# A tuned float32 layer kernel: its warm-up reads a constant, gate's weight comes in two loads, and the first products go by halves of the inputs

## The chip, the cores and the metric

The kernel runs on one core of one Trainium2 chip. The metric is the device time of one execution in microseconds (us). The kernel before took 528.29 us, the median of three runs (527.94 to 528.46).

## The reference

The input `x` is (4, 2048, 256) in float32, so 8192 tokens of 256 features. A layer is chunked linear attention with a gate, a residual and a layer norm, and then a gated feed-forward network with integer weights, a residual and a second layer norm. Cut to what is computed:

```python
Q, K, V = x @ W_q.T, x @ W_k.T, x @ W_v.T
mask = where(diff >= 0, decay ** diff, 0)          # inside chunks of 32 tokens; decay = sigmoid(log_decay[0])
S = einsum('bncd,bnkd->bnck', Qc, Kc) * mask
O = einsum('bnck,bnkd->bncd', S, Vc).reshape(B, T, D)
gate = sigmoid(x @ W_g.T)
x = layernorm(x + (gate * O @ W_o.T + x))          # attention adds its own x as well
h = silu(x @ wg.T) * (x @ wu.T)                    # wg, wu, wd: integers of -127..127, times 1/127
x = layernorm(x + h @ wd.T)
```

## The kernel before

The 8192 tokens are worked on in 16 blocks of 512 (`TB`). Activations are held with the features in the partitions (`xT`, two chunks of 128 features by 512 tokens) for the products, and with the tokens in the partitions for the norms. The scores use the product M of W_q and W_k (`m_sb`, made once by `make_m`), so that one projection `yT` takes the place of Q and K. From block 1 on, gate, y, v and the output projection are split into seven half-size products (`seven`, `split_gate`, `token_sums`, `weight_sums`), with the sums of quarters made by GpSimd. The feed-forward products use the weights in two kinds, as float32r (`hi`) and float16 (`lo`). The last two blocks have a hand-written tail. A branch at the end, `wide_block`, handles integers too large for float16; with these inputs it is not entered, though it calls `attn_gate` too.

The work of all blocks is overlapped in one long program per engine. A scheduler puts the instructions of each engine in order; those given to `in_turn` (`tc.keep_in_program_order`) keep the order of the program.

What matters here is the head, before the loop over the blocks begins at line 938:

- **Loads.** `load_w(nc.scalar, w_gT, "wg")` (line 138) issues gate's weight, 256 KB, as the first instruction of ScalarE's queue. On SyncE's queue (SP) `load_xT(0, pieces=KD)` issues block 0's `xT` in two loads of 256 KB, one for each chunk of 128 features. Behind `wg` on ScalarE's queue stand `wv`, `decay` and `wk`; behind `xT_0` on SP stand `wq`, `xT_1` (512 KB), `wo`, the two blocks of `x` and nine pieces of the integer weights. The loads from SP and ScalarE share eight completion semaphores, which are given out in turn; a load that takes one again waits for the load that had it.
- **Warm-up.** Lines 174 to 178: VectorE writes a tile `idle` of 128 by 512 zeros, and TensorE multiplies it twice (`WARM`) into a bank that nobody reads. Each float32 product appears in the trace as two pieces.
- **First products.** `attn_gate(0)` (line 889) makes gate of block 0: for each half `dc` of the output features, two products over the input chunks `ec`, then ScalarE's sigmoid of that bank. `attn_v(0)` follows with `wv`, then `make_m` with `wq` and `wk`, then `split_gate(1, x_sums)`, whose sums GpSimd makes from `xT_1`, and `attn_y(0)`.
- **Sigmoid of decay.** ScalarE's first computing instruction is the sigmoid of `decay` (line 205); the sigmoids of gate stand behind it on that engine. VectorE builds the mask from `decay`.

Constants such as zeros are also there without a tile of the kernel's own: the program's first instructions, GpSimd memsets ahead of the barrier that starts all engines, lay down one column of each.

Of the kernel before, what the change touches and what calls it, by code (L numbers as in the profile page):

```python
# [47 lines left out]
F32 = mybir.dt.float32  # L48
# [6 lines left out]
P = 128  # L55
# [3 lines left out]
TB = 512  # L59
# [12 lines left out]
def kernel(  # L72
# [15 lines left out]
    nc = tc.nc  # L88
    NT, D = x.shape
    H = ffn_gT.shape[1]  # L90
    KD = D // P
# [4 lines left out]
    const = ctx.enter_context(tc.tile_pool(name="const", bufs=1))  # L96
# [12 lines left out]
    def bank(name):  # L109
        return psum.tile([P, TB], F32, tag="ps", name=name)  # L110
# [5 lines left out]
    def load_xT(b, start=None, pieces=1):  # L116
        xt = xin.tile([P, KD, TB], F32, tag="xT", name=f"xT_{b}")
        src = xT[:, span(b, start)].rearrange("(k p) t -> p k t", p=P)
        n = KD // pieces
        for k in range(0, KD, n):  # L120
            nc.sync.dma_start(xt[:, k : k + n, :], src[:, k : k + n, :])
        return xt
# [3 lines left out]
        nc.sync.dma_start(xn, x[span(b, start), :].rearrange("(g p) d -> p g d", p=P))  # L126
        return xn

    def load_w(eng, w, name):
        k, n = w.shape[0] // P, w.shape[1]  # L130
        t = const.tile([P, k, n], w.dtype, tag=name, name=name)
        eng.dma_start(t, w.rearrange("(k p) n -> p k n", p=P))
        return t


    decay = const.tile([P, 1], F32, tag="decay", name="decay")
    xTs, xns = {}, {}
    wg = load_w(nc.scalar, w_gT, "wg")
    xTs[0] = load_xT(0, pieces=KD)
    wv = load_w(nc.scalar, w_vT, "wv")  # L140
    nc.scalar.dma_start(decay, log_decay[0:1, 0:1].to_broadcast([P, 1]))
    wq = load_w(nc.sync, w_q, "wq")
    wk = load_w(nc.scalar, w_k, "wk")
    xTs[1] = load_xT(1)
# [26 lines left out]
    ]  # L171


    idle = const.tile([P, TB], F32, tag="idle", name="idle")
    nc.vector.memset(idle, 0.0)
    pi = bank("pi")
    for _ in range(WARM):
        nc.tensor.matmul(pi, lhsT=idle[:, :P], rhs=idle, start=True, stop=True)  # L178

    ident = const.tile([P, P], F32, tag="ident", name="ident")  # L180
    make_identity(nc, ident)
# [108 lines left out]
    def in_turn(ins):  # L290
        tc.keep_in_program_order(ins)
# [260 lines left out]
    def attn_gate(b):  # L552
        xt = xTs[b]
        sg = work.tile([P, KD, TB], F32, tag="sg", name=f"sg_{b}")
        for dc in range(KD):
            pg = bank(f"pg_{b}_{dc}")
            for ec in range(KD):
                nc.tensor.matmul(  # L558
                    pg,
                    lhsT=wg[:, ec, dc * P : (dc + 1) * P],  # L560
                    rhs=xt[:, ec, :],
                    start=(ec == 0),
                    stop=(ec == KD - 1),
                )
            nc.scalar.activation(sg[:, dc, :], pg, AF.Sigmoid)
        return sg

# [245 lines left out]
    def ffn_down(b, uT, h, between=None, chunkwise=False):  # L813


        r = work.tile([P, NG, D], F32, tag="r2", name=f"r2_{b}")
        mv = no_moments(f"f{b}")
        made = None
        order = in_turn if chunkwise else free

        def residual(gs, pb):

            order(
                nc.vector.scalar_tensor_tensor(  # L824
                    flat(r, gs), pb, SCALE**3 / U_UP * H_UP, flat(h, gs), ALU.mult, ALU.add
                )
            )
            nonlocal made
            moments(r, f"f{b}", range(gs.start, gs.stop), order, mv)
            if between is not None and gs.start == 0:  # L830
                made = between()

        ws = [chunked(w) for w in fd]
        if chunkwise:
            per = TB // D
            banks = [bank(f"fdn_{b}_{k}") for k in range(NG // per)]
            for late, terms in enumerate(early_and_late(uT, ws)):
                for k, pb in enumerate(banks):
                    for i, (part, w) in enumerate(terms):
                        for j in range(per):  # L840
                            g = k * per + j
                            product = nc.tensor.matmul(  # L842
                                pb[:, j * D : (j + 1) * D],
                                lhsT=part[:, g * P : (g + 1) * P],
                                rhs=w,
                                start=late + i + j == 0,
                                stop=True,
                                skip_group_check=True,
                            )
                            in_turn(product)  # L850
                    if late:
                        residual(slice(k * per, (k + 1) * per), pb)
        else:
            project_back(b, uT, ws, residual, "fdn")
        return r, mv, made
# [31 lines left out]
    table = const.tile([P, 1], F32, tag="table", name="table")  # L887
    hs, hTs = {}, {}
    sg, v = attn_gate(0), attn_v(0)
    for w, name in ((wg, "g"), (wv, "v")):  # L890
        w_sums[name] = weight_sums(w, name)
# [46 lines left out]
    for b in range(NB - 2):  # L938
        n = b + 2
# [67 lines left out]
        else:  # L1007
# [14 lines left out]
            r_out, mv_out, _ = ffn_down(b, uT, hs.pop(b), chunkwise=True)  # L1022
# [6 lines left out]
    per = NG // 2  # L1029
# [26 lines left out]
    r_before, mv_before, _ = ffn_down(last - 1, uT, hs[last - 1], chunkwise=True)  # L1056
# [28 lines left out]
    banks = [bank(f"fdn_{last}_{g}")[:, :D] for g in range(NG)]  # L1085
# [42 lines left out]
    def wide_block(start, weights):  # L1128

        wide_g, wide_u, wide_d = weights  # L1130
        xTs["w"] = load_xT("w", start)
        xns["w"] = load_xn("w", start)
        sg, v = attn_gate("w"), attn_v("w")
        goT = attn_values("w", attn_scores("w", attn_y("w")), v, sg)
        h = attn_out("w", goT)
# [41 lines left out]
    with tc.If(wide_any > 0):  # L1177
# [10 lines left out]
        for w in (ffn_gT, ffn_uT, ffn_dT):  # L1188
            weights.append([])
            for src in int_pieces(w):  # L1190
                t = room.pop(0).rearrange("p (k n) -> p k n", n=D)
# [47 lines left out]
```

## Time and profile before

| | |
|---|---|
| median of 3 runs | 528.29 us (527.94 to 528.46) |
| the profiled execution, its time | 527.63 us |
| its span in the profile | 525.9 us |
| granted TensorE clock, mean | 0.995 |
| TensorE busy from 0 to 60 us, outside of the first 1.45 | all of it |
| TensorE busy from 500 to 525.9 us | 18.74 of 25.90 us |
| weight `wg`: issue, time to landing | 0.73 us, 4.4 us |
| `xT_0`, first half | 0.73 us, 3.7 us |
| `xT_0`, second half | 1.18 us, 4.7 us |
| `xT_1` | 2.11 us, 8.8 us |
| `wk` | 2.26 us, 8.9 us |

The span is what the profile shows from the first to the last instruction; the time of a run includes 1.73 us around it. PE is TensorE's matmuls, PEld its weight loads, DVE VectorE, ACT ScalarE, POOL GpSimd and SP SyncE. Start times are us from the beginning of the span. The times to landing are those from the start of a load's issue to the moment all of its data is there.

### The profile page before, as it was taken

What the parts mean: (1) busy time and instruction counts of PE and PEld (TensorE: products, weight loads), DVE (VectorE), ACT (ScalarE), POOL (GpSimd) and SP (SyncE); (2) the same over time, 40 slices, a digit from 0 to 9 for tenths busy, and PEclk for the clock granted to TensorE, in tenths of its full rate; (3) what the DMA queues carried; (4) which work ended last, traced back from release to release, by engine and by line L of the source; (5) the groups of instructions that cost most, each with busy time, mean ns of one, the idle gap of its engine ahead of it and who ended that gap; (6) DMA issues with size and microseconds to landing.
All of it is one profiled execution on the core that took longest, in us unless ns stands there. A gap on an engine that the chain in (4) does not pass through costs nothing.

```text
span 525.9 us, 10552 instructions
## 1 busy us (share of the span) xinstructions
PE 517.3 (98%) x3646; PEld 422.2 (80%) x3646; DVE 389.8 (74%) x964; ACT 322.3 (61%) x644; POOL 343.2 (65%) x476
## 2 busy tenths in 40 slices
PE   8999999999999999999999999999999999999994
PEld 5798887887978788887887978788887888878683
DVE  3878797686786867777677776867868677787865
ACT  2745565465656756666575655666666575667744
POOL 6535785766847668585776857668485675735653
PEclk9999999999999999999999999999999999999998
DMA  7721121213213131131312313141131312011201
GB/s 252 218 91 42 51 60 28 65 42 67 96 34 87 53 110 41 39 109 31 105 42 51 112 30 92 49 113 41 36 93 51 105 42 53 30 27 54 79 22 65
DMA packets 43256, 36.90 MB, mean 70 GB/s; under 512 B 4800, under 2 KB 39104, under 8 KB 43200
## 3 DMA queue, kind: packets, MB, share of 16 engines
q1 hardware_dynamic: 42240, 35.41, 23.2%
q8 instruction: 30, 0.49, 0.4%
q10 hardware_dynamic: 960, 0.79, 0.4%
q14 instruction: 26, 0.21, 0.2%
HBM read 20.45 MB, written 8.39 MB: 55 GB/s over the span
## 4 chain that ended last, share of the span: by engine, by line
PE 95%; DVE 2%; ACT 1%; POOL 1%; issue 0%; DVEq 0%; ACTq 0%
PE fg L776 16%; PE fu L776 16%; PE fdn L663 14%; PE p_v L462 9%; PE p_y L444 9%; PE p_g L444 9%; PE p_o L462 8%; PE po L637 5%; PE ps L616 3%; PE fdn L842 2%; PE pa L663 1%; PE pg L558 1%; PE pi L178 1%; PE pv L596 1%; PE py L575 1%; DVE st_f L311 0%
## 5 line engine op out<-in xcount | busy, mean ns | idle before, releaser
L801 POOL TENSOR_TENSOR u_lo<-u,u_hi 128x512 f16<-128x512 f32 (+1 forms) x98 | 123.0, 1257 | 111.0 <-ACT u_hi L800 109.6
L800 ACT CAST u_hi<-u 128x512 fp32r<-128x512 f32 (+1 forms) x98 | 59.7, 609 | 65.3 <-DVE u L798 64.9
L786 DVE SCALAR_TENSOR_TENSOR s<-fg,s 128x512 f32<-128x512 f32 (+1 forms) x98 | 65.9, 673 | 34.3 <-ACT s L784 34.1
L784 ACT ACTIVATE s<-fg 128x512 f32<-128x512 f32 (+1 forms) x98 | 56.9, 583 | 41.5 <-PE fg L776 41.4
L798 DVE TENSOR_TENSOR u<-fu,s 128x512 f32<-128x512 f32 (+1 forms) x98 | 66.4, 678 | 10.4 <-POOL u_lo L801 1.1
L776 PE MATMUL fg<-hT_hi,fg_hi 128*128 128x512 f32 (+1 forms) x196 | 74.0, 458 | 0.0
L776 PE MATMUL fu<-hT_hi,fu_hi 128*128 128x512 f32 (+1 forms) x196 | 60.5, 390 | 0.0
L776 PE MATMUL fg<-hT_lo,fg_lo 128*128 128x512 f16 (+1 forms) x196 | 58.0, 377 | 0.0
L776 PE MATMUL fu<-hT_lo,fu_lo 128*128 128x512 f16 (+1 forms) x196 | 57.4, 375 | 0.0
L663 PE MATMUL fdn<-fd_hi,u_hi 128*128 128x256 f32 x312 | 46.9, 292 | 0.0
L776 PEld LDWEIGHTS fu<-hT_hi,fu_hi 128*128 128x128 f32 x196 | 36.5, 188 | 8.5
L399 ACT ACTIVATE h<-h,shift_h,scale_h 128x256 f32<-128x256 f32 x52 | 27.0, 590 | 24.1 <-POOL shift_h L362 24.1
L776 PEld LDWEIGHTS fg<-hT_hi,fg_hi 128*128 128x128 f32 x196 | 34.6, 189 | 8.8
L663 PEld LDWEIGHTS fdn<-fd_hi,u_hi 128*128 128x128 f32 x312 | 39.8, 189 | 0.3
L663 PE MATMUL fdn<-fd_lo,u_lo 128*128 128x256 f16 x312 | 38.6, 273 | 0.0
L776 PEld LDWEIGHTS <-fu_lo 128*128 128x128 f16 x196 | 19.2, 98 | 22.2
L824 DVE SCALAR_TENSOR_TENSOR r<-fdn,h 128x512 f32<-128x512 f32 x30 | 20.7, 689 | 21.6 <-PE fdn L663 19.1
L759 POOL TENSOR_TENSOR hT_lo<-hT,hT_hi 128x512 f16<-128x512 f32 x28 | 35.3, 1280 | 1.2 <-ACT hT_hi L758 1.2
L776 PEld LDWEIGHTS <-fg_lo 128*128 128x128 f16 x196 | 15.3, 98 | 20.7 <-issue 12.9
L663 PEld LDWEIGHTS <-u_lo 128*128 128x128 f16 x312 | 28.4, 98 | 4.2
L462 PE MATMUL p_v<-v_sums,x_sums 128*128 128x128 f32 x240 | 31.7, 275 | 0.0
L637 PE MATMUL po<-sT,v 128*128 128x128 f32 x256 | 31.2, 275 | 0.0
(207 smaller groups left out, 1183.0 us busy)
## 6 DMA issues: line engine op xcount, KB each, us to landing
x<-in_x_dram SPq DMA_DIRECT2D x16, 512.0 KB, 3.5
xT<-in_xT_dram SPq DMA_DIRECT2D x15, 512.0 KB, 4.3
hT<-sq SPq DMA_DIRECT2D x224, 32.0 KB, 1.9
out_dram<-r SPq DMA_DIRECT2D x14, 512.0 KB, 5.0
fg_int<-in_ffn_gT_dram SPq DMA_DIRECT2D x3, 256.0 KB, 7.8
fu_int<-in_ffn_uT_dram SPq DMA_DIRECT2D x3, 256.0 KB, 7.0
fd_int<-in_ffn_dT_dram SPq DMA_DIRECT2D x3, 256.0 KB, 5.9
xT<-in_xT_dram SPq DMA_DIRECT2D x2, 256.0 KB, 4.2
```

The lines of the kernel that those rows point to most:

```text
L399: nc.scalar.activation(r[:, g, :], r[:, g, :], AF.Identity, bias=shift[:, g : g + 1], scale=scale[:, g : g + 1],)
L444: nc.tensor.matmul(pb, lhsT=a[i - 1], rhs=b[i - 1], start=first, stop=True, skip_group_check=True,)
L462: nc.tensor.matmul(pb[:, g * P : (g + 1) * P], lhsT=b[i - 1][:, g * P : (g + 1) * P], rhs=a[i - 1], start=first and g == 0, stop=True, ski ...
L637: nc.tensor.matmul(po[:, cols], lhsT=v[:, g, dc * P : (dc + 1) * P], rhs=sT[:, cols], start=True, stop=True,)
L663: nc.tensor.matmul(pb[:, j * D : (j + 1) * D], lhsT=part[:, g * P : (g + 1) * P], rhs=w, start=(i == 0), stop=(i == len(terms) - 1),)
L759: nc.gpsimd.tensor_tensor(in_order[1], whole, in_order[0].bitcast(F32), ALU.subtract)
L776: nc.tensor.matmul(pb, lhsT=w[kind][:, dc, hc * P : (hc + 1) * P], rhs=hT[kind][:, dc, cols], start=(kind == kinds[0] and dc == 0), stop=( ...
L784: order(nc.scalar.activation(s, pg, AF.Sigmoid, scale=SCALE / H_UP))
L786: gated = nc.vector.scalar_tensor_tensor(s, pg, U_UP / H_UP**2, s, ALU.mult, ALU.mult)
L798: in_steady_turn(nc.vector.tensor_tensor(u, pu, s, ALU.mult))
L800: nc.scalar.copy(hi, u)
L801: nc.gpsimd.tensor_tensor(lo, u, hi.bitcast(F32), ALU.subtract)
```

## The change

Three edits. `load_w` takes a number of pieces, and gate's weight is issued as two loads of 128 KB, one for each input chunk. The tile `idle` and its memset are gone; both operands of the warm-up products read the constant zero, one element repeated over the free dimension. In `attn_gate` the loop over the input chunks becomes the outer one: both banks get the product of the first chunk, then both get that of the second, in this order on TensorE; the two sigmoids come after all four products.

```diff
-    def load_w(eng, w, name):
+    def load_w(eng, w, name, pieces=1):
         k, n = w.shape[0] // P, w.shape[1]
         t = const.tile([P, k, n], w.dtype, tag=name, name=name)
-        eng.dma_start(t, w.rearrange("(k p) n -> p k n", p=P))
+        per = k // pieces
+        for i in range(0, k, per):
+            eng.dma_start(
+                t[:, i : i + per, :], w.rearrange("(k p) n -> p k n", p=P)[:, i : i + per, :]
+            )
         return t
...
-    wg = load_w(nc.scalar, w_gT, "wg")
+    wg = load_w(nc.scalar, w_gT, "wg", pieces=KD)
...
-    idle = const.tile([P, TB], F32, tag="idle", name="idle")
-    nc.vector.memset(idle, 0.0)
     pi = bank("pi")
     for _ in range(WARM):
-        nc.tensor.matmul(pi, lhsT=idle[:, :P], rhs=idle, start=True, stop=True)
+        nc.tensor.matmul(
+            pi,
+            lhsT=nc.const_aps.tensor(0.0, [P, P]),
+            rhs=nc.const_aps.tensor(0.0, [P, TB]),
+            start=True,
+            stop=True,
+        )
...
-        for dc in range(KD):
-            pg = bank(f"pg_{b}_{dc}")
-            for ec in range(KD):
-                nc.tensor.matmul(
+        banks = [bank(f"pg_{b}_{dc}") for dc in range(KD)]
+
+        for ec in range(KD):
+            for dc, pg in enumerate(banks):
+                product = nc.tensor.matmul(
                     pg,
                     lhsT=wg[:, ec, dc * P : (dc + 1) * P],
                     rhs=xt[:, ec, :],
                     start=(ec == 0),
                     stop=(ec == KD - 1),
                 )
+                in_turn(product)
+        for dc, pg in enumerate(banks):
             nc.scalar.activation(sg[:, dc, :], pg, AF.Sigmoid)
```

On each engine the order of instructions is otherwise that of before. One thing follows from the extra load without being in the diff: with eight semaphores in turn, the ninth load of the program, the first that takes one again, was `wo` and is now `xT_1`.

## The prediction

> **What bounds the kernel now.** I read the page first (busy shares, then the chain that ended last), then the chain in order of time over the first 20 us, the windows, and last the head instruction by instruction. In the page the reader sees TensorE busy for 98% of the span and carrying 95% of the chain:
>
> ```profile
> span 525.9 us, 10552 instructions
> PE 517.3 (98%) x3646; PEld 422.2 (80%) x3646; DVE 389.8 (74%) x964; ACT 322.3 (61%) x644; POOL 343.2 (65%) x476
> PE 95%; DVE 2%; ACT 1%; POOL 1%; issue 0%; DVEq 0%; ACTq 0%
> ```
>
> In the windows (stretch, its length, then busy time of PE, PEld, DVE, ACT, POOL) PE's busy time equals the length of the stretch: after 1.45 us TensorE has no gap until the tail.
>
> ```profile
> 1.45:5.23 3.78, 3.78 (x5) 1.21 (x5) 0.24 (x2) 1.28 (x1) 1.44 (x6) 1.00 0.84 266
> 5.23:9.10 3.87, 3.87 (x9) 1.94 (x10) 0.07 (x1) 0.30 (x2) 3.87 (x9) 1.00 0.68 209
> 60.00:500.00 440.00, 440.00 (x3126) 360.89 (x3125) 332.28 (x801) 278.04 (x551) 295.95 (x391) 1.00 0.22 62
> ```
>
> The chain in order of time (start, length, what) says what TensorE does first. Only the 0.72 us before the start, the memset of `idle` and the warm-up lie ahead of real work:
>
> ```profile
> 0.72 0.18 issue
> 0.91 0.50 DVE idle L175
> 1.40 0.04 issue
> 1.45 3.78 PE pi L178 x4
> 5.23 3.83 PE pg L558 x8
> 9.06 3.45 PE pv L596 x16
> 12.52 1.73 PE pm L194 x8
> ```
>
> The timeline of the head shows that the first real weight load waits for a transfer and not for the warm-up (in brackets: idle time before, and releaser):
>
> ```profile
> 2.46 0.34 PEld L178 LDWEIGHTS pi<-idle 128*128 128x128 f32 x1 [0.52 <-issue]
> 3.32 0.34 PEld L178 LDWEIGHTS pi<-idle 128*128 128x128 f32 x1 [0.52 <-issue]
> 5.19 0.47 PEld L558 LDWEIGHTS pg<-xT,wg 128*128 128x128 f32 x2 [1.54 <-DMA wg<-in_w_gT_dram]
> 5.90 0.19 PEld L558 LDWEIGHTS pg<-xT,wg 128*128 128x128 f32 x1 [0.24 <-DMA xT<-in_xT_dram]
> 10.99 0.85 POOL L433 TENSOR_TENSOR x_sums<-xT 128x256 f32<-128x256 f32 x1 [1.38 <-DMA xT<-in_xT_dram]
> ```
>
> A float32 product is two pieces on the array. The warm-up's four start at 1.45, 2.46, 3.31 and 4.17, 0.86 apart, so the array is through at 4.17 + 0.86 = 5.03. The weight `wg` lands 4.4 us after its issue at 0.73, at 5.13, and the first load starts at 5.19. From there the eight gate pieces come 0.43 apart. Landing times of the others, issue plus time to landing: first half of `xT_0` 0.73 + 3.7 = 4.43, second half 1.18 + 4.7 = 5.88, `wv` 6.52, `wq` 8.74, `decay` 8.74, `xT_1` 10.91, `wk` 11.16.
>
> **What the Trainium skill says.** "TensorE: Matmul & The Clock Gate", Part 1: The HAM clock gate: an idle array runs at half clock and is released after a busy window of 3413 ns, and the window is free-running, so the moment varies between executions. The trace agrees in kind: 0.86 us a piece first, 0.43 later. The first gate weight load took 302 ns where cold ones took 338 and warm ones 190, so the clock rose at about 5.45, 4.0 us after TensorE's first work. "DMA: Bandwidth & Descriptors", Queues, rings and completion order: the queues of SyncE and ScalarE each have a ring on the same 16 engines, which take turns between them packet by packet. The trace agrees: `wg` and the halves of `xT_0` move side by side at 353 GB/s together from 3.25 to 5.75. The pages price no matmul operand that reads one element over and over.
>
> **The change, part by part.**
>
> *Warm-up from the constant.* POOL writes the constant at 0.25, ahead of the start barrier, so nothing after 0.72 holds the warm-up back. Its start is 0.72 plus TensorE's own issue: 0.76 with the 0.04 of the chain, 0.91 if it is as slow as VectorE. I take 0.85, 0.60 earlier. Four pieces then end at 0.85 + 3.58 = 4.43. The repeated read of one element is not in the trace: not faster, since the array clock sets 0.86; at worst twice 0.86, which would end the warm-up near 7.9. I take 0.86, because the number of columns is the same and the values are zeros in both; the other end is left to the chance of slower. VectorE loses a memset of 0.48 us in front of 7.34 us of idleness (its next work waits for `decay`): nothing.
>
> *Gate's weight in two loads.* At 353 GB/s shared by two queues a load gets about 176 GB/s, so the second 128 KB take 0.74 us, and the first half lands at 5.13 - 0.74 = 4.39 (bounds 4.1 and 4.8). The second still lands near 5.13. One more issue on ScalarE's queue, 0.4 to 0.5 us, moves `wv`, `decay` and `wk` back in issue by that much. Their landings are set by the ring, which is busy until well after their issue, so I take 0.1 (0 to 0.45). Behind the issues stand the table load (1.28 us at 2.75, then 4.76 us idle) and the sigmoid of `decay`; the gate's sigmoids stand behind that one, at 8.99. Cover: `wv` is needed at about 7.9; `wk` at 12.14 - 0.6 = 11.54 against 11.16, so 0.38 us is free.
>
> *An indirect wait.* Each load takes one of eight completion semaphores in turn. Before, the ninth load was `wo`, which waits for the first load and so went out at 5.17. With one load more the ninth is `xT_1`: the list of waits of the changed kernel shows it behind semaphore 0, which is the first half of `wg`. Its issue moves from 2.11 to about 4.45, and on SP `wo`, both `x` and nine weight pieces stand behind it. But its data waited anyway: it follows `wq` in SP's ring, and `wq` lands at 8.74. Issue to first data was about 1 us for the first load, so descriptors are there at 5.5, in time. I take 0; bounds 0 and 2.34 (the whole issue delay). GpSimd's sums (four of some 0.75 us) hang on it. The product that needs the third of them, ready at 13.26, would come at 13.9: 0.64 us are free. `wo` and what follows go out within 0.3 us of before.
>
> *Products by halves.* Same eight pieces, same order on the engine afterwards. The first four need only the first halves: max(4.43 warm-up, 4.43 `xT_0`, 4.39 `wg`) + 0.06 = 4.49 instead of 5.19, saving 0.70. The other four come 1.7 us or more later, after 5.88. Both sigmoids now follow all eight pieces, finished by about 8.3, and wait for `decay` at 8.74 as before: nothing.
>
> *Clock.* The exposed cold weight load stays, so products stream from 4.80. If the clock rises 4.0 us after the start again (4.85), they lose 0.03; if it rises at 5.45 as before, they are cold for 0.65 us and lose half, 0.33. Sum: 0.67 or 0.37. I take 0.55, nearer the first, because the execution shown lost next to nothing to cold products and a random window treats both kernels alike.
>
> Profiled execution: 525.9 - 0.55 = 525.35 span; with the 1.73 around it (527.63 - 525.9) 527.1. The median, 528.29, lies 0.66 above that execution, so the forecast is 528.29 - 0.55 = **527.7**. About 0.2% (1.06 us) is what a measurement of this kernel can tell from no change, so this counts as no change.
>
> **Rivals.**
>
> *The gain is swallowed (528.2).* The clock rises where it did and `wk` lands 0.4 late. For: only 0.38 us of cover. Against: ring and not issue sets landings. 0.37 less a wait of some 0.3 leaves 0.1.
>
> *Clearly faster (526.9).* If the weight load is hidden and all pieces are warm, gate ends at 4.49 + 8 x 0.43 = 7.93 instead of 8.90, a gain of 0.97; and the median's surplus of 0.66 may be cold products, which an earlier warm-up removes in part. 0.97 + 0.4 gives 1.4. Against: it wants a lucky clock, and `xT_0` at 4.43 and `wk` at 11.16 cap it.
>
> *Slower (529.4): `xT_1` behind the new wait.* If its landing moves by the whole 2.34, x_sums' consumer stalls 2.34 - 0.64 - 0.6 (already gained) = 1.1 beyond the old time. It decides from a delay of 1.24, where the kernel is even; slower by 0.2% needs 2.3. For: DMA share falls to 0.38 between 5.75 and 7.50, so the rings do run dry there. Against: in that stretch `wq` and `decay` are ahead of it.
>
> *The warm-up doesn't do its work*, because it reads one zero: the first products run cold, or the warm-up itself lasts to 7.9; either costs 1 to 3 us and is part of the chance of slower.
>
> **How the numbers follow.** Forecast 0.56, swallowed 0.15, faster 0.20, slower 0.09. The first two are within 0.2%: 0.71. Range 526.9 to 528.7: it takes in the swallowed case, the bounds 0.37 and 0.97, a few tenths of spread between executions (527.94 to 528.46 shown), and the nearer half of the faster case; the slower case stays out.
>
> **What would show it.** First warm-up piece near 0.85 and released by no memset; first gate load near 4.5 with `wg` or `xT` as releaser; `pv` from about 8.2 to 8.5 instead of 8.90; `pm` near 11.6 without a wait for `wk`; `xT_1` issued near 4.45, landing by 11; PE without gaps later. Wrong if `x_sums` starts after 12, if gate pieces stay 0.86 apart past 6, or if PE shows idle time between 9 and 15.

## The result, and the profile after

The changed kernel takes 527.20 us (median of 22 runs, 526.65 to 528.07) against 528.06 for the kernel before, measured beside it (22 runs, 527.29 to 528.87). The ratio is 0.9986 with a 95% interval of 0.998 to 0.9992: 0.74 us won, between 0.42 and 1.06. (The two medians alone are 0.86 apart; gains are given here by the ratio.) A second measurement of the same kernel (e4 below) gave 0.9985 (0.9978 to 0.9991). So the gain is real, at about 0.14%.

The one profile of after, taken alone, seems to say the opposite. Its page:

```profile
span 526.3 us, 10554 instructions
PE 517.9 (98%) x3646; PEld 422.4 (80%) x3646; DVE 390.1 (74%) x963; ACT 322.3 (61%) x644; POOL 342.5 (65%) x476
```

The span is 0.4 us longer than that of before. The chain in order of time (start, length, what) shows where the head stands:

```profile
0.67 0.06 issue
0.73 3.89 DMA wg<-in_w_gT_dram
4.62 0.04 issue
4.66 4.53 PE pg L567 x8
9.20 3.45 PE pv L607 x16
12.65 1.73 PE pm L202 x8
```

The memset and the warm-up have left the chain: it now begins with the first half of gate's weight, which lands at 4.62. (In other profiles of kernels with this head, such as those of e3 and e4, it begins with the warm-up: the two end within a few tenths of a microsecond of each other.) Gate's products follow it at 4.66, 0.53 us earlier than before (5.19). But they take 4.53 us instead of 3.83, so `pv` starts at 9.20, 0.14 later than before (9.06). The weight loads in the timeline say why:

```profile
0.74 0.50 PEld L180 LDWEIGHTS pi<-const-float32-0.0 128*128 128x128 f32 x2 [0.74 <-issue]
1.76 0.34 PEld L180 LDWEIGHTS pi<-const-float32-0.0 128*128 128x128 f32 x1 [0.52 <-issue]
2.61 0.34 PEld L180 LDWEIGHTS pi<-const-float32-0.0 128*128 128x128 f32 x1 [0.52 <-issue]
4.66 0.50 PEld L567 LDWEIGHTS pg<-xT,wg 128*128 128x128 f32 x2 [1.72 <-DMA wg<-in_w_gT_dram]
5.68 0.34 PEld L567 LDWEIGHTS pg<-xT,wg 128*128 128x128 f32 x1 [0.52 <-issue]
6.46 0.19 PEld L567 LDWEIGHTS pg<-xT,wg 128*128 128x128 f32 x1 [0.44 <-issue]
6.89 0.19 PEld L567 LDWEIGHTS pg<-xT,wg 128*128 128x128 f32 x1 [0.24 <-issue]
```

A load of 0.34 us is one at half clock, one of 0.19 at full clock. The warm-up starts at 0.74 to 0.77 instead of 1.45, and its pieces are 0.86 apart with the constant as with the tile. In this execution the clock rose near 6.3 us. In the profiled execution of before it rose near 5.6: the line `5.19 0.47`, shown in the prediction, covers two loads, and the one that took 302 ns is the second of them, from 5.36 to 5.66; it was at half clock for about 0.26 us of that (0.338 us is a cold load, 0.190 a warm one). Real work was thus cold (at half clock) for some 1.3 us here, from 5.0 to 6.3, and for next to nothing there. After the head the windows show TensorE without a gap, as before:

```profile
30.00:60.00 30.00, 30.00 (x239) 25.43 (x238) 22.88 (x61) 16.61 (x36) 19.07 (x30) 1.00 0.22 72
60.00:500.00 440.00, 440.00 (x3125) 360.92 (x3125) 332.16 (x802) 278.05 (x552) 295.56 (x391) 1.00 0.22 62
```

The chain gives a ruler for all runs of this study. From the start of `py` in it to the start of the last normalising instruction on VectorE (line 875 of before, 886 of after) it is 504.83 us in before and 504.77 in after. The two lines of before, then those of after:

```profile
15.97 3.43 PE py L575 x8
520.80 0.41 DVE r L875
```

```profile
16.10 3.43 PE py L586 x8
520.87 0.41 DVE r L886
```

In the other nine profiles whose chain runs over `py` it is 504.77 to 504.82. What the head wins or loses arrives at the end to within 0.06 us. The rest of the scatter lies behind it: from that instruction to the end of the timed run it is 6.8 to 7.6 us, in code that the change leaves as it was.

### The profile page after: what moved, and what is told of

Same layout as the page of the kernel before. It is cut to its first block, busy times and chain, and to the rows that moved or that the text cites. A ratio compares the mean times of both kernels' runs of the same rounds, so it can differ in the third digit from the quotient of the medians.

```text
span 526.3 us, 10554 instructions
## 1 busy us (share of the span) xinstructions
PE 517.9 (98%) x3646; PEld 422.4 (80%) x3646; DVE 390.1 (74%) x963; ACT 322.3 (61%) x644; POOL 342.5 (65%) x476
## 4 chain that ended last, share of the span: by engine, by line
PE 95%; DVE 2%; ACT 1%; DMA 1%; POOL 1%; issue 0%; DVEq 0%; ACTq 0%
PE fg L787 16%; PE fu L787 15%; PE fdn L674 14%; PE p_v L470 9%; PE p_y L452 9%; PE p_g L452 9%; PE p_o L470 8%; PE po L648 5%; PE ps L627 3%; PE fdn L853 2%; PE pa L674 1%; PE pg L567 1%; DMA wg<-in_w_gT_dram 1%; PE pv L607 1%; PE py L586 1%; DVE st_f L319 0%
```

## The experiments

"Won" is one minus the ratio, times 528. Each line has its own interval of the ratio to before, which was measured beside it each time: its median was 528.06 beside e1 to e4 too, 528.37 beside e5 to e8 and 528.15 beside e10 and e11, so rows are to be compared by the ratio. The last columns are from the one profile of each, in us: the start of gate's first weight load, the start of `pv` (gate's end, but in e7 and e11, where `pv` waits for `wv`) and of `py` in the chain. In e10 the chain does not run over `pv` and `py`.

| | median, runs | ratio to before (95%) | first gate load | `pv` | `py` |
|---|---|---|---|---|---|
| before | 528.06, 22 | 1 | 5.19 | 9.06 | 15.97 |
| changed | 527.20, 22 | 0.9986 (0.998 to 0.9992) | 4.66 | 9.20 | 16.10 |
| e1 constant only | 527.43, 13 | 0.9994 (0.9986 to 1.0002) | 4.65 | 9.27 | 16.18 |
| e2 loads and halves only | 528.04, 14 | 0.9996 (0.9987 to 1.0005) | 4.17 | 9.45 | 16.36 |
| e3 gate in the old order | 527.29, 21 | 0.9988 (0.9981 to 0.9994) | 4.08 | 8.33 | 15.53 |
| e4 changed again | 527.20, 21 | 0.9985 (0.9978 to 0.9991) | 4.25 | 8.65 | 15.56 |
| e5 no warm-up | 529.40, 9 | 1.0025 (1.0015 to 1.0035) | 4.51 | 9.63 | 16.53 |
| e6 three warm-up products | 527.94, 21 | 0.9994 (0.9987 to 1.0) | 5.12 | 9.14 | 16.05 |
| e7 decay from GpSimd | 529.03, 9 | 1.0016 (1.0006 to 1.0026) | 4.34 | 9.65 | 16.83 |
| e8 one warm-up product | 529.64, 15 | 1.0025 (1.0017 to 1.0032) | 4.52 | 9.86 | 16.77 |
| e10 decay in rows | 527.84, 13 | 0.9994 (0.9986 to 1.0002) | 4.15 | - | - |
| e11 xT_1 before wq | 528.34, 13 | 1.0001 (0.9993 to 1.001) | 4.12 | 9.47 | 16.64 |

**e4: the changed kernel a second time.** No edit.

> The changed kernel once more, for a second profile of it. Theory: the clock rises at another moment than in the first profile (about 6.3 us), anywhere from 4.2 to 7.6, and pv starts later by half of what lies between that moment and 4.97; the time of the profiled execution follows. Rival (the clock rises a fixed time after TensorE's first work): again near 6.3, and pv again at 9.03.

The same four warm-up pieces at the same times, and then:

```profile
4.25 0.50 PEld L567 LDWEIGHTS pg<-xT,wg 128*128 128x128 f32 x2 [1.30 <-DMA wg<-in_w_gT_dram]
5.27 0.33 PEld L567 LDWEIGHTS pg<-xT,wg 128*128 128x128 f32 x1 [0.52 <-issue]
5.92 0.19 PEld L567 LDWEIGHTS pg<-xT,wg 128*128 128x128 f32 x1 [0.32 <-issue]
6.35 0.19 PEld L567 LDWEIGHTS pg<-xT,wg 128*128 128x128 f32 x1 [0.24 <-issue]
```

Here the weight landed at 4.2 and the clock rose near 5.7, so `pv` starts at 8.65: the same program, 0.55 us earlier than in its first profile, and 0.41 earlier than before. The profiled execution took 527.58 us, that of the first profile 528.03. The fixed-delay rival is out: with TensorE's first work at 0.77 or 0.78 in every case the clock rose near 5.1 (e3), 5.7 (e4), 6.3 (the first profile) and 6.6 (e11). In e7 and e10 gate's first loads were at full clock already:

```profile
4.34 0.30 PEld L567 LDWEIGHTS pg<-xT,wg 128*128 128x128 f32 x2 [1.38 <-DMA wg<-in_w_gT_dram]
```

```profile
4.15 0.30 PEld L568 LDWEIGHTS pg<-xT,wg 128*128 128x128 f32 x2 [1.21 <-DMA wg<-in_w_gT_dram]
```

There it rose while the last warm-up piece ran: the four pieces took 3.36 us in e7 and 3.52 in e10, against 3.75 where the whole warm-up was cold, which puts the rise near 3.6 and 3.9 (estimates from these lengths).

**e1 and e2: half of the change each.** e1 puts only the constant into the kernel before; e2 takes it out of the changed one.

```diff
-    idle = const.tile([P, TB], F32, tag="idle", name="idle")
-    nc.vector.memset(idle, 0.0)
...
-        nc.tensor.matmul(pi, lhsT=idle[:, :P], rhs=idle, start=True, stop=True)
+        nc.tensor.matmul(
+            pi,
+            lhsT=nc.const_aps.tensor(0.0, [P, P]),
+            rhs=nc.const_aps.tensor(0.0, [P, TB]),
...
```

> The kernel before with the warm-up from the constant alone: one load of gate's weight, products in the old order. Theory (the start of the first product sets the head, and the clock rises at a moment that is free against the program): the warm-up starts near 0.77 us but the first gate load still waits for the whole weight, 5.1 us; the clock rises 0.68 us earlier on average, so 0.2 to 0.3 us are won. Rival A (the earlier warm-up carries the change): the whole gain of about 0.75 us. Rival B (the loads carry it): no gain.

> The changed kernel with the old warm-up (tile and memset of VectorE). Theory: the first half of the weight lands at 4.6 us, the warm-up is through at 5.03, so the first product streams at about 5.05 instead of 5.46, but still as cold as before: 0.2 to 0.3 us won. Rival A: nothing won. Rival B: about 0.75 us won.

e1 won 0.3 us and e2 0.2, both as the theory had it, though the interval of each includes no change. Rival A expected 0.75 in e1 and rival B in e2: the first is just inside e1's interval (0.0014 against 0.0014), the second is outside of e2's (0.0013 at most). So these two runs speak against B and leave A at the edge. What speaks against A is the trace, where e1's first gate load still waits for the whole weight:

```profile
4.65 0.50 PEld L562 LDWEIGHTS pg<-xT,wg 128*128 128x128 f32 x2 [1.70 <-DMA wg<-in_w_gT_dram]
```

In this execution the whole weight landed at 4.61, as early as its first half did in the profile of after. What the split is worth has to be read from all profiles: the first half landed between 4.0 and 4.6 in ten of them, the whole weight at 5.13 and 4.61 in two. e2's timeline shows the other half of the argument:

```profile
3.31 0.34 PEld L182 LDWEIGHTS pi<-idle 128*128 128x128 f32 x1 [0.52 <-issue]
4.17 0.34 PEld L563 LDWEIGHTS pg<-xT,wg 128*128 128x128 f32 x1 [0.52 <-DMA wg<-in_w_gT_dram]
5.02 0.34 PEld L563 LDWEIGHTS pg<-xT,wg 128*128 128x128 f32 x1 [0.52 <-issue]
```

The weight is there by 4.1 and its load is hidden, but the old warm-up holds the array until 5.03. The start of real work is the later of the two, so that each half of the change should be worth little without the other. That the whole is more than the sum of the halves (0.74 against 0.5) follows from this, but the intervals are too wide to show it.

**e3: gate in the old order.** The changed kernel with the loops of `attn_gate` as before.

```diff
-        for ec in range(KD):
-            for dc, pg in enumerate(banks):
+        for dc in range(KD):
+            pg = bank(f"pg_{b}_{dc}")
+            for ec in range(KD):
...
```

> The changed kernel with gate's products in the old order (by halves of the outputs); the weight still comes in two loads. Theory: the second half of xT_0 lands at 5.4 and of the weight at 5.7, and two cold pieces last from 4.97 to 6.7 (two warm ones to 5.8), so the second product is hardly held up: within 0.1 us of the changed kernel, 0.65 to 0.85 us faster than before. Rival (the order by halves is what lets the first products start early): at most 0.4 us faster than before.

The two sigmoids go back between the products, and the products are no longer held in turn. It won 0.63 us (0.3 to 1.0), next to the changed kernel's 0.74. The rival's 0.4 is not wholly excluded, but its mechanism does not appear:

```profile
4.08 0.57 PEld L566 LDWEIGHTS pg<-xT,wg 128*128 128x128 f32 x2 [1.13 <-DMA wg<-in_w_gT_dram]
5.16 0.19 PEld L566 LDWEIGHTS pg<-xT,wg 128*128 128x128 f32 x1 [0.51 <-DMA wg<-in_w_gT_dram]
```

The second product's weight load stands at 5.16, one cold piece after the product before it, when the other half of the weight has just landed (1.17 + 3.9 = 5.07). Two cold pieces of the first half last long enough; the order by halves is worth some 0.1 us by the ratios, and nothing that this profile shows. Gate ends early in this profile, which shows what comes next:

```profile
13.13 0.41 PEld L452 LDWEIGHTS p_g<-xT,wg 128*128 128x128 f32 x2
13.96 1.16 PEld L452 LDWEIGHTS p_g<-x_sums,g_sums 128*128 128x128 f32 x6 [0.42 <-POOL x_sums L443]
```

`pv` starts 0.73 earlier than before, but `py` only 0.44: 0.29 is lost where TensorE waits for GpSimd's sums of `xT_1`, which had landed at about 11.6.

**e5, e8 and e6: no, one and three warm-up products.** `WARM` is 0, 1 and 3.

> The changed kernel with no warm-up products at all. Theory (the clock rises one to two windows[...] after TensorE's first work, and each us of cold products costs half of it): the first products stream at about 4.5 and run cold until 7.6 to 11.1, on average 4.8 us, so gate and v end 2.4 us later than warm ones and 1.7 us later than in the changed kernel: 0.9 us slower than before. Rival (the clock does not hang on the warm-up, the gain is that of the loads): as fast as the changed kernel.

> The changed kernel with one warm-up product: TensorE works from 0.77 to 2.6 and then idles until 4.2 to 4.7. Theory: what raises the clock is a window filled with work, so after the pause the count begins anew and the time is that of no warm-up, about 0.9 us slower than before. Rival (any early work counts): the clock rises as in the changed kernel, and the time is the changed kernel's.

> The changed kernel with three warm-up products in place of two, so that the clock has more often risen when real work begins. Theory: TensorE has 14 pieces without a pause from 0.9 us on, two more than in the changed kernel, half of them cold on average: 0.7 us slower than the changed kernel, about even with before. Rival (cold first products are the larger loss, a longer warm-up pays): faster than the changed kernel by 0.2 us or more.

e5 is 1.3 us slower than before, so the warm-up is worth about 2.1 us in the changed kernel (1.0025 against 0.9986). In its profile the clock rose near 7.4:

```profile
4.51 0.50 PEld L558 LDWEIGHTS pg<-xT,wg 128*128 128x128 f32 x2 [4.51 <-DMA wg<-in_w_gT_dram]
7.24 0.27 PEld L558 LDWEIGHTS pg<-xT,wg 128*128 128x128 f32 x1 [0.52 <-issue]
7.75 0.19 PEld L558 LDWEIGHTS pg<-xT,wg 128*128 128x128 f32 x1 [0.24 <-issue]
```

e8 gives the same 1.3: one product, then a pause from 2.6 to 4.5, is worth nothing. Whether that is because of the pause, or because 1.8 us of work are too short in any case, is not separated. In its profile the loads stay at 0.34 us until 7.24 and are 0.19 from 7.98 on:

```profile
4.52 0.50 PEld L567 LDWEIGHTS pg<-xT,wg 128*128 128x128 f32 x2 [3.28 <-DMA wg<-in_w_gT_dram]
5.54 0.34 PEld L567 LDWEIGHTS pg<-xT,wg 128*128 128x128 f32 x1 [0.52 <-issue]
6.39 0.34 PEld L567 LDWEIGHTS pg<-xT,wg 128*128 128x128 f32 x1 [0.52 <-issue]
7.24 0.34 PEld L567 LDWEIGHTS pg<-xT,wg 128*128 128x128 f32 x1 [0.52 <-issue]
7.98 0.19 PEld L567 LDWEIGHTS pg<-xT,wg 128*128 128x128 f32 x1 [0.40 <-issue]
```

Both rivals fall. The cost came out above the 0.9 expected, which the intervals just allow. e6 won 0.3 us against before, 0.4 less than the changed kernel: the theory had 0.7 less, and the rival's gain is outside of the interval. The chain of e6:

```profile
0.77 4.94 PE pi L180 x6
5.71 3.43 PE pg L567 x8
```

A longer warm-up does not pay, since the array still works on zeros when the data is there: the weight's first half landed at 4.6, and the first product of gate follows at 5.55 in the timeline (the chain counts to the end of the piece before it). In this profile all eight pieces of gate were warm, and `pv` still started at 9.14. Two products end about when the weight comes.

**e7, e11 and e10: the loads behind.** The two open questions were whether the wait of `xT_1` for a semaphore takes back part of the gain, and what holds `xT_1` up. e7 issues `decay` from GpSimd, which leaves eight loads ahead, so that `xT_1` does not wait; e11 issues `xT_1` ahead of `wq`; e10 loads a row of 128 numbers in place of 4 bytes. The three edits in this order, that of e10 cut:

```diff
-    nc.scalar.dma_start(decay, log_decay[0:1, 0:1].to_broadcast([P, 1]))
+    nc.gpsimd.dma_start(decay, log_decay[0:1, 0:1].to_broadcast([P, 1]))
...
+    xTs[1] = load_xT(1)
     wq = load_w(nc.sync, w_q, "wq")
     wk = load_w(nc.scalar, w_k, "wk")
-    xTs[1] = load_xT(1)
...
-    nc.scalar.dma_start(decay, log_decay[0:1, 0:1].to_broadcast([P, 1]))
+    nc.scalar.dma_start(decay_row, log_decay[0:1, 0:P].to_broadcast([P, P]))
```

> The changed kernel with the load of decay (128 pieces of 4 bytes) issued by GpSimd, which takes no semaphore of the eight: xT_1 is the eighth load again and does not wait. Theory: the wait for the semaphore is harmless, since xT_1 landed at 10.7 to 11.6 with it and at 10.9 to 11.9 without it; what xT_1's landing does cost is the wait for x_sums in executions whose gate ends before 8.6, of 0.3 us in one of two. Within 0.2 us of the changed kernel. Rival (the indirect wait took back part of the gain): faster than the changed kernel by 0.3 us or more, with xT_1 landing before 10.

> The changed kernel with xT_1 issued ahead of wq on SP, so that xT_1 does not wait for a semaphore and wq does. Theory (the indirect wait is harmless, since xT_1 was limited by what moved ahead of it): xT_1 lands earlier, at 8 to 9.5, and wq later, at 8 to 10, before the 11.5 at which it is needed; x_sums' wait of about 0.3 us in one of two executions goes: 0 to 0.2 us faster than the changed kernel. Rival (the semaphore's wait is a loss of its own): 0.3 us or more faster. Other end: wq lands after 11.5 and TensorE waits for it.

> The changed kernel with decay loaded as a row of 128 numbers into each partition (512 bytes each; the first is used) instead of 4 bytes each, in the same place of ScalarE's queue. Theory (the 4-byte pieces hold up the engines between 5.75 and 7.5 us, and what stands behind them sets x_sums): the DMA stays above 300 GB/s from 3.25 on, decay lands before 7.5, xT_1 a microsecond earlier, before 9.8, and x_sums no longer makes TensorE wait in any execution. Worth 0.1 to 0.2 us against the changed kernel, so 0.9 us faster than before. Rival (the low stretch comes from the wait of xT_1 for its semaphore and from issue, not from decay): the stretch stays, and nothing is won.

All three missed the time expected. Without its wait `xT_1` does not come early by itself: it lands at 11.4 in e7 (2.1 + 9.3), later than the 10.7 of the changed kernel. In e11, where it also goes ahead of `wq`, it lands at 8.9 (1.6 + 7.3), as expected, and the kernel is slower all the same. What comes late in both is `wv`, and TensorE waits for it. The lines are from the timelines of e7 and e11:

```profile
9.65 3.32 PEld L607 LDWEIGHTS pv<-wv,xT 128*128 128x128 f32 x16 [2.44 <-DMA wv<-in_w_vT_dram]
```

```profile
9.47 3.32 PEld L607 LDWEIGHTS pv<-wv,xT 128*128 128x128 f32 x16 [1.24 <-DMA wv<-in_w_vT_dram]
```

`wv` lands 7.9 and 7.8 us after its issue, against 5.3 in the changed kernel and 4.8 to 6.0 in all other profiles. So no run shows the wait of `xT_1` taking anything back; the two versions without it were 1.6 and 0.8 us slower than the changed one. Nor does the missing wait alone make `wv` late: in before and in e1 `xT_1` does not wait either, and `wv` landed at 6.5 and 6.0. There it was issued at 1.22, ahead of SP's load of 1.64; in e7 and e11 it was issued at 1.67 and 1.65, beside it. Which of these differences counts is not settled, since e7 also moves `decay` and e11 also moves `wq`.

In e10 the low stretch of the DMA stays. The windows of the changed kernel (its first profile, then e4) and of e10 from 5.75 to 7.50 us (the last two columns are DMA share and GB/s):

```profile
5.75:7.50 1.75, 1.75 (x5) 0.83 (x4) 0.00 (x0) 0.00 (x0) 1.74 (x4) 1.00 0.61 171
```

```profile
5.75:7.50 1.75, 1.75 (x5) 0.76 (x4) 0.00 (x0) 0.00 (x0) 1.75 (x6) 1.00 0.52 123
```

```profile
5.75:7.50 1.75, 1.75 (x5) 0.76 (x4) 0.00 (x0) 0.00 (x0) 1.75 (x5) 1.00 0.45 115
```

With pieces of 512 bytes in place of 4 the stretch is no fuller, so the 4-byte pieces are not its cause. The larger load of `decay` lands at 9.13 instead of 8.14, VectorE's work on the mask starts later by as much, and the chain now runs over that work. The weight loads of the products with x_sums wait 0.66 us, though gate ended at 7.69 in this profile, earlier than in any other. What empties the queues in that stretch is open.

No version of these beats the changed kernel.

## Why the prediction was right

It named no change beyond 0.2%, 0.55 us won and 527.7 us; measured were 0.74 (0.42 to 1.06) and 527.20. Of the 0.5 us between forecast and measured median 0.23 is the kernel before, which took 528.06 beside the changed one and not 528.29. By its steps:

- *Warm-up from the constant.* Taken at 0.85, bounds 0.76 and 0.91; it is 0.77. The price of a piece that reads one element was open; it is 0.86, the value taken.
- *Gate's weight in two loads.* First half estimated at 4.39 (4.1 to 4.8). The profile of after has 4.62, the others with two loads 4.0 to 4.6. The same load is not as steady as the prediction treated it: the whole weight landed at 5.13 in before and at 4.61 in e1. One term here was too small: the extra issue was to set `wv`'s landing back by 0.1 (at most 0.45), and `wv` landed at 6.95 in after and about 7.7 in e3, against 6.5 in before. It cost nothing, because `pv` needs it only when gate ends, but in e3 the first weight load of `pv`, at 7.74, came just behind it. The reason given, that the ring and not the issue sets the landings, is not borne out for `wv`.
- *First product.* Its weight load was expected at 4.49; it is seen at 4.66, 4.25 and 4.08 (changed, e4, e3). In e4 and e3 the product itself waited for the end of the warm-up, at 4.31 in their timelines, as the prediction's sum has it with the start of 0.77.
- *The indirect wait.* `xT_1` was issued at 4.64 and landed at 10.74, before it was 10.91. Taken at zero, and so it is. The cover behind it, put at 0.64 us, is real but not always there: in e3 TensorE lost 0.29 on it. `wk`, feared late, came at 8.97 instead of 11.16.
- *Products by halves.* The prediction charged the 0.70 us of earlier start to this step. In e3 the early start is there without it, from the two loads and the warm-up; the order adds some 0.1 by the ratios.
- *Clock.* This is the term that was mis-sized. It was bounded by 0.03 and 0.33 us lost, from a rise at 4.85 or at 5.45. The 5.45 was misread: the load of 302 ns is the second, and the rise was near 5.6. (For the same reason the pieces of gate come 0.43 apart only from the second on.) The rises seen with the earlier warm-up lie anywhere from about 3.6 to 6.6, and the profile of after lost some 0.65. For one pair of profiles the sum 525.35 was wrong even in sign (526.3). For medians the term should nearly cancel, as the sentence on a random window said, because it strikes both kernels; then 0.67 is left of the sum, close to the 0.74 measured. No run separates the term from the rest, and both 0.55 and 0.67 lie within the interval, so the closeness of either is in part luck.

The Trainium skill ("TensorE: Matmul & The Clock Gate", Part 1: The HAM clock gate) says that the window is free-running and that the moment of the rise varies. e4 beside the first profile shows it. The slower rival did not occur; where kernels of this study did get slower by the loads, in e7 and e11, it was by `wv` and not by `xT_1`. The faster rival's 1.4 us lie outside of the interval; it wanted an early rise in the median, and over many runs the rises scatter.

## What to carry to other kernels

- The head of a kernel whose matrix engine never pauses is worth its full length: find the later of the warm-up's end and the first operand's landing, and move both, since one alone bought little here (0.3 and 0.2 us against 0.74). The warm-up was long enough here when it ended as the data landed: a third product cost 0.4 us, and a single one with a pause behind it was worth nothing.
- A gain of a few tenths of a microsecond is not to be read from one pair of profiles when the clock's rise is free against the program. Take the size of a gain from many runs and the mechanism from the profiles.
- When a load is split, count which later load now waits for a completion semaphore; and before that wait is taken away, look at what lands late without it.

## What the runs showed of the hardware that was not expected

- With no warm-up (e5) the clock rose near 7.4, 2.9 us after TensorE's first work at 4.51. With it the delay was shortest in e7, about 2.8 us (0.78 to near 3.6), and longest in e11, about 5.8 (0.77 to near 6.6). A busy window of 3.4 us, as the Trainium skill has it ("TensorE: Matmul & The Clock Gate", Part 1: The HAM clock gate), is therefore not needed in full; how much of it is needed is open.
- A matmul whose two operands repeat one element over the free dimension takes the time of one that reads a whole tile: 0.86 us a piece at half clock, with zeros in both (after and before).
- The landing of a load issued first of all at 0.73 us varied between executions: by 0.4 us for the same program (128 KB: 4.62 in after, 4.21 in e4), and by 0.5 for the same loads in two programs (256 KB: 5.13 in before, 4.61 in e1). That of `wv` went from 6.95 to 9.42 when the loads of the other queue were put in another order (e11).
